# A graph network with attention on one core: the output's base traced behind the next softmax, and loads of bias rows tied to a step of the attention

## The chip, the cores and the metric

The kernel runs on one core of a Trainium2 chip. The metric is the device time of one execution in microseconds (us). A core has five engines that run their own instruction streams and wait for each other through semaphores: TensorE (PE, with its weight loads as PEld), VectorE (DVE), ScalarE (ACT), GpSimd (POOL) and SyncE (SP), which here issues nearly all DMAs and does nothing else. An engine takes its instructions in the order of the program, so one that waits holds up all that stand behind it on the same engine; on SP a DMA issue that waits holds up the issues behind it.

## The reference

What is computed is a graph network with pre-normalised attention over N = 1024 nodes of D = 512 features, in float32. Cut to what matters:

```
h = relu(layernorm(x))
x_in = h
h = batchnorm(h); h = gcn(h, gcn_in_w) + gcn_in_b
for i in range(4):
    a = attention(ln2(h), cond, Wq[i], Wk[i], Wv[i], Wo[i])   # 16 batches of 64 nodes, 256 keys each, 8 heads
    h = h + a
    val, gate = split(ln3(h) @ geglu_w[i] + geglu_b[i])
    h = h + (val * gelu(gate)) @ ffo_w[i] + ffo_b[i]
h = gcn(h, gcn_out_w) + gcn_out_b
return x + h + x_in
```

The change deals with two things of small arithmetic. One is the base of the output, `x + gcn_out_b + relu(layernorm(x))`, to which the last graph product is added at the very end. It doesn't depend on the layers, so it can be made at any time; two of its eight blocks of 128 nodes are made in each of the four layers. The other is the bias row `ffo_b[i]`, which is added to h once in each layer.

## The kernel before

The nodes are eight blocks of 128 (`h[0]` to `h[7]`). The attention of a layer runs over eight groups g of 128 nodes, two batches each. Products of large matrices are made from three products of twelve-bit parts: a left side x is split into a high part (`ah`, by ACT), a low part (`al`, by DVE) and a third (`as`, by POOL, in two halves); a bank of PSUM takes the first two products, ACT scales the bank, and then PE adds the third product. So the third product of each block k or v (L370) waits for ACT's scaling of its bank (L381).

In the loop over g, iteration g does, in the order of the source:

- `fetch_x`, in iterations 1 and 2 alone: loads a block of x again (`x_again`, L1550), and the first time in each layer also the row `bias_out` (by `load_row`, L136);
- the keys of group g + 1 and the mixing of group g, which turns its probabilities on PE (`tr_pr`), then the scores and the softmax of group g + 1 (`scores`): 32 small products into four banks, then for each bank the negative maximum `nmax` on DVE (L838), two exponentials on ACT (L843), a reciprocal and two scalings on DVE (L848). `scores.last` is the last of these scalings;
- the rest of mixing: `ol` and `os` on DVE (L892, L893), traced behind `scores.last` by `tc.issue_after`;
- `base_of`, in iterations 1 and 2 alone: `again` on ACT (L1556), two adds on DVE (L1558, L1559), and a store of the block to `base_dram` (L1560);
- the load of the condition of group g + 3 and its split for group g + 2 (`ah_c`, `al_c`, `as_c`), the values of group g + 1, and the output product of the attention of group g (`oy`, `ox`), which is added to `h[g]`. In layer 0 alone the condition is loaded raw in four pieces (`cond`, L270), turned on PE at the end of the iteration (`tr_cond`) and stored (`cond_dram`, L276) for the other layers, which load it turned (`ct`, L283).

Iteration 6 also loads the weights of the gated part (`wval`, `wgate`, L126), and `add_bias` loads the row `ffb` (L136) and adds it to h. POOL's sums of these weights (`ges`) wait for `scores.last`. The feed-forward part follows: gated products, whose results go to DRAM (`f_dram`), and the output product (`fy`, `fx`, L1252), which loads them back (`fr`) with the weights (`wff`).

The order in which the instructions stand on an engine is not that of the source. A scheduler makes it out of dependencies and of its own estimates, and may pull work ahead of where it was written. Three helpers bind it: `pin` keeps PE's products in program order; `tc.issue_after(i)` puts what is traced on the engine of i behind i, with no semaphore; `waiting_for(i, engine)` makes each instruction that is traced on that engine wait for i by a semaphore.

In the order that it makes, the first base block of a layer stands on DVE ahead of the softmax of group 1, in iteration 0, and the second inside or right behind that softmax, though both were written two iterations later. The loads of `bias_out` and `ffb` stand on SP much ahead too: those of layer 0 at the start of the program, those of layers 1 to 3 in the feed-forward part of the layer before.

Of the kernel before, what the change touches and what calls it, by code (L numbers as in the profile page):

```python
# [26 lines left out]
def gnn_kernel(  # L27
# [29 lines left out]
    N, D = x.shape  # L57
# [27 lines left out]
    @contextmanager  # L85
    def waiting_for(ins, engine):

        traced = nc.cur_bb.bb.instructions
        n = len(traced)
        yield  # L90
        for i in traced[n:]:
            if i.engine == engine:
                tc.add_manual_dep(i, ins.ins.name, mybir.DependencyInfo(
                    mybir.DependencyClass.Sync, mybir.DependencyReason.DATA))
# [36 lines left out]
    def three_halves(name):  # L131
        return rows.tile([P, 3 * D // 2], F32, tag="gs2", name=name, bufs=2)

    def load_row(vec, offset, name, t=None):
        t = three_halves(name)[:, :D] if t is None else t
        nc.sync.dma_start(  # L136
            t, bass.AP(tensor=vec.tensor, offset=vec.offset + offset, ap=[[0, P], [1, D]])
        )
        return t
# [665 lines left out]
    def acc_tile(name):  # L805
        return accs.tile([P, 512], F32, tag="acc", name=name)
# [13 lines left out]
    def scores(l, g, qT, kT):  # L820


        c0 = (g % 4) * P
        probs = {}
        banks = [bank(f"sc_{l}_{g}_{u}") for u in range(4)]
        for c2 in range(2):
            for a in range(2):
                for j in range(2):
                    pj = slice(j * DH, (j + 1) * DH)
                    for b in range(2):  # L830
                        pin(nc.tensor.matmul(
                            banks[2 * c2 + j][b * NPG:(b + 1) * NPG, a * M:(a + 1) * M],
                            qT[g // 4][c2][pj, a, c0 + b * NPG:c0 + (b + 1) * NPG],
                            kT[c2][pj, a, b * M:(b + 1) * M], start=True, stop=True))
        for u in range(4):
            ps3 = banks[u].rearrange("p (a m) -> p a m", a=2)
            nmax = small.tile([P, 2], F32, tag="nmax", name=f"nmax_{l}_{g}_{u}")
            nc.vector.tensor_reduce(nmax, ps3, AX.X, OP.max, negate=True)  # L838
            pr = t512(f"pr_{l}_{g}_{u}")
            pr3 = pr.rearrange("p (a m) -> p a m", a=2)  # L840
            tot = small.tile([P, 2], F32, tag="tot", name=f"tot_{l}_{g}_{u}")
            for a in range(2):
                nc.scalar.activation(pr3[:, a, :], ps3[:, a, :], AF.Exp,  # L843
                                     bias=nmax[:, a:a + 1], accum_out=tot[:, a:a + 1])
            inv = small.tile([P, 2], F32, tag="inv", name=f"inv_{l}_{g}_{u}")
            nc.vector.reciprocal(inv, tot)
            for a in range(2):
                scores.last = nc.vector.tensor_scalar(pr3[:, a, :], pr3[:, a, :], inv[:, a:a + 1],  # L848
                                                      None, OP.mult)
            probs[u] = pr  # L850
        return probs
# [85 lines left out]
    def load_geglu(l, r):  # L937
        return [load_w(geglu_w[l][:, r * D:(r + 1) * D], f"wval_{l}_{r}"),
                load_w(geglu_w[l][:, DFF + r * D:DFF + (r + 1) * D], f"wgate_{l}_{r}")]

    def geglu_weights(l, r, wval, wgate):
        s = slots_of(3, f"ges_{l}_{r}")
        sums_of_a(nc.gpsimd, *wval, *wgate, *s)
        return order7([*wval, *wgate], *s)
# [480 lines left out]
    for l in range(L):  # L1425
# [90 lines left out]
        def take_ln3():  # L1516
            ln3T.extend(slots_of(2, f"ln3T_{l}_{i}") for i in range(2))
            ln3S.extend(slots_of(3, f"ln3S_{l}"))
            right.extend([ln3T[0][0], ln3T[0][1], ln3T[1][1], ln3S[2], ln3S[0], ln3S[1],
                          ln3T[1][0]])  # L1520
# [22 lines left out]
        fetched = {}  # L1543

        def fetch_x(nb):
            if not fetched:
                fetched["bias"] = three_halves(f"bias_out_{l}")[:, :D]
                load_row(gcn_out_b, 0, "bias_out", fetched["bias"])
            fetched[nb] = acc_tile(f"x_again_{nb}")
            nc.sync.dma_start(fetched[nb], x[nb * P:(nb + 1) * P, :])  # L1550

        def base_of(nb):


            xt, bias_out, xn = fetched.pop(nb), fetched["bias"], acc_tile(f"again_{nb}")
            nc.scalar.activation(xn, xt, AF.Relu, bias=x_shift[:, nb:nb + 1],  # L1556
                                 scale=x_root[:, nb:nb + 1])
            nc.vector.tensor_tensor(xt, xt, bias_out, OP.add)  # L1558
            nc.vector.tensor_tensor(xt, xt, xn, OP.add)  # L1559
            nc.sync.dma_start(base_dram[nb], xt)  # L1560

        ffb = []

        def add_bias(t, *blocks):
            if not ffb:
                ffb.append(load_row(ffo_b, l * D, f"ffb_{l}"))
            for nb in blocks:
                t.tensor_tensor(h[nb], h[nb], ffb[0], OP.add)

# [11 lines left out]
        for g in range(NG - 1):  # L1581
            if g == NG - 2:
                take_ln3()
                raw = load_geglu(l, 0)
                add_bias(nc.vector)
            if not g:
                probs = scores(l, g, qT, kTs.pop(g))
            if g == NG - 2:
                with waiting_for(scores.last, mybir.EngineType.Pool):
                    left = geglu_weights(l, 0, *raw)  # L1590
            wo_flow = out_parts(l, wo) if not g else iter(())
            wo = next(wo_flow, wo)
            if g in (1, 2):
                fetch_x(2 * l + g - 1)
            k = keys(l, g + 1, wk, 1 if l == 0 and g == 0 else 0)
            for i, u in enumerate(k):
                u.begin()
                if not i:
                    for end in ends:
                        end()  # L1600
                if i > 1:
                    k[i - 2].end()
                next(wo_flow, None)
            k[-2].end()
            for _ in wo_flow:
                pass
            v = values(l, g + 1, wv)
            with in_order(mybir.EngineType.DVE) if g == NG - 2 else nullcontext():
                oT = mix(l, g, probs, vs.pop(g), (
                    k[-1].end, nothing, lambda: (v[0].begin(), g == NG - 2 and  # L1610
                                                 add_bias(nc.vector, *range(4)))))
            if g < NG - 2:
                probs = scores(l, g + 1, qT, kTs.pop(g + 1))
                with tc.issue_after(scores.last.ins):
                    oT = oT()
            if g == NG - 2:
                oT = oT()
                ln3_norm(g - 2, g - 1, behind=mix.last)
                add_bias(nc.gpsimd, g - 2, g - 1)
            if g in (1, 2):  # L1620
                base_of(2 * l + g - 1)
            if l == 0:
                fetch_cond(g + 3)
            split_cond(l, g + 2)
            if l:
                load_cond(l, g + 3)
            v[1].begin()
            v[0].end()
            v[2].begin()
            v[1].end()  # L1630
            pieces = attn_out(l, g, oT, wo, pin) if g < NG - 2 else iter(())
            next(pieces, None)
            if g in (3, 5):
                moments_into(mv_kept[:, 2 * (g - 3):2 * (g - 1)], [h[g - 3], h[g - 2]],
                             f"ln3_{l}_{g - 3}")
            if g == NG - 2:
                for nb in range(4):
                    ln3_turn(nb, each=pin)
            v[3].begin()
            next(pieces, None)  # L1640
            v[2].end()
            next(pieces, None)
            ends = [v[3].end]
            if g == NG - 3:
                scale_kept()
            if g == NG - 2:
                for nb in range(4, 6):
                    ln3_turn(nb, each=pin)
                for nb in (g - 2, g - 1):
                    ln3_sums(nc.gpsimd, nb)  # L1650
            if l == 0 and g + 3 < NG:
                turn_cond(g + 3, each=pin)
        g = NG - 1
        f, quads = quads_of(l, 0, left, right)
# [109 lines left out]
        for r in range(1, R):  # L1764
            f = Gated(l, r)
# [189 lines left out]
```

## Time and profile before

| | |
|---|---|
| median of 3 runs | 2304.32 us (2302.94 to 2304.63) |
| profiled execution, its own time | 2308.55 us |
| profiled execution, span of its instructions | 2306.8 us |
| mean granted clock of PE in it | 0.998 |
| DVE busy | 1738.5 us (75%) |
| ACT busy | 1169.6 us (51%) |
| POOL busy | 750.3 us (33%) |
| packets of SP's DMA queue | 25.8% of 16 engines' span |

The profile is of one execution on the chip, and its span starts at its first instruction. In a row of the order of time stand the start, the duration, the engine, the line of the kernel, the operation and the tiles that it writes and reads; xN counts merged instructions, and square brackets hold the idle time of the engine before it with what ended it. The ends of PE's products are modelled, so its busy time is not its peak. A row of a stretch has its length and each engine's busy time, with counts. A row of waits has the sum, the count and the longest.

### The profile page before, as it was taken

The numbers are of one execution on the slowest core, as the hardware profiler recorded it, in microseconds if no ns is written. First come the engines' busy times: TensorE is split into PE (matmuls) and PEld (weight loads), VectorE is DVE, ScalarE is ACT, GpSimd is POOL, SyncE is SP. The second block draws the span as 40 slices with busy tenths as digits, with TensorE's granted clock in tenths as the row PEclk, the third lists the DMA queues.
The fourth block names the chain that finished last, engine by engine and source line by source line (L and its number), as shares of the span: only waits on it lengthen the run. The fifth ranks groups of instructions, "written<-read, shape, count | busy, mean of one in ns | idle before, by whom it ended". The sixth has DMA issues, their size and how long they took to land. (4 is left out here: it accounts for less than half of the span.)

```text
span 2306.8 us, 34462 instructions
## 1 busy us (share of the span) xinstructions
PE 2271.7 (98%) x12496; PEld 1757.1 (76%) x12496; DVE 1738.5 (75%) x3172; ACT 1169.6 (51%) x2245; POOL 750.3 (33%) x647
## 2 busy tenths in 40 slices
PE   8999999999999999999999999999999999999999
PEld 5677887587887888488787888578788788668777
DVE  9886556999986556989987554989988554899965
ACT  7555445465355445465356444556437444556521
POOL 1121213486022224377022222368112113168301
PEclk9999999999999999999999999999999999999999
DMA  7042211234512101133522111133531111043551
GB/s 214 2 151 70 69 62 36 82 119 146 183 46 74 47 28 37 60 122 96 209 91 74 38 38 38 38 109 101 192 137 51 41 47 46 1 128 110 183 171 59
DMA packets 144114, 204.42 MB, mean 89 GB/s; under 512 B 11241, under 2 KB 68913, under 8 KB 143937
## 3 DMA queue, kind: packets, MB, share of 16 engines
q1 hardware_dynamic: 141840, 196.72, 25.8%
q0 software_dynamic: 1376, 4.30, 0.6%
q8 instruction: 103, 1.69, 0.3%
q10 hardware_dynamic: 720, 1.11, 0.1%
q14 instruction: 75, 0.61, 0.1%
HBM read 151.75 MB, written 50.34 MB: 88 GB/s over the span
## 5 line engine op out<-in xcount | busy, mean ns | idle before, releaser
L324 POOL TENSOR_TENSOR as_c<-ah_c,al_c 128x512 fp32r<-128x512 f32 x128 | 200.4, 1595 | 906.6 <-DVE al_c L319 711.3
L1123 ACT ACTIVATE g<-g 128x512 f32<-128x512 f32 x192 | 112.4, 585 | 152.3 <-PE g L1109 150.7
L381 ACT ACTIVATE k<-k 128x512 f32<-128x512 f32 x125 | 73.0, 586 | 197.9 <-PE k L370 197.9
L1252 PE MATMUL fy<-bl_wff,al_f 128*128 128x512 f32 x512 | 160.1, 392 | 1.3 <-DVE bl_wff L1229 0.8
L318 ACT ACTIVATE ah_f<-fr 128x1024 fp32r<-128x1024 f32 x64 | 67.9, 1061 | 183.7 <-PE fy L1252 90.7
L1252 PE MATMUL fx<-bs_wff,as_f 128*128 128x512 f32 x512 | 160.4, 393 | 0.6 <-DVE as_f L321 0.6
L1252 PE MATMUL fy<-bh_wff,ah_f 128*128 128x512 f32 x512 | 158.4, 391 | 0.2 <-ACT ah_f L318 0.2
L386 DVE COPY kT<-k 128x512 f32<-128x512 f32 x54 | 37.2, 689 | 156.6 <-PE k L370 156.6
L370 PE MATMUL v<-bs_wv,as_c 128*128 128x512 f32 x508 | 137.4, 393 | 7.2 <-ACT v L381 7.2
L370 PE MATMUL v<-bh_wv,ah_c 128*128 128x512 f32 x508 | 141.2, 400 | 0.0
L1050 POOL TENSOR_TENSOR gsa<-gha,gla 128x512 fp32r<-128x512 f32 x96 | 124.2, 1315 | 40.2 <-DVE gla L1045 40.2
L843 ACT ACTIVATE pr<-sc,nmax 128x256 f32<-128x256 f32 x256 | 118.2, 476 | 37.3 <-DVE nmax L838 36.7
L370 PE MATMUL v<-bl_wv,al_c 128*128 128x512 f32 x508 | 136.4, 390 | 0.0
L370 PE MATMUL k<-ah_c,bh_wk 128*128 128x512 f32 x500 | 135.0, 392 | 0.0
L381 ACT ACTIVATE v<-v 128x512 f32<-128x512 f32 x127 | 75.2, 592 | 116.9 <-PE v L370 116.9
L370 PE MATMUL k<-as_c,bs_wk 128*128 128x512 f32 x500 | 132.1, 395 | 1.7 <-ACT k L381 1.7
L370 PE MATMUL k<-al_c,bl_wk 128*128 128x512 f32 x500 | 133.7, 389 | 0.0
L1109 PE MATMUL g<-gr,gha 128*128 128x512 f32 x384 | 120.0, 394 | 0.0
L1109 PE MATMUL g<-gr,gsa 128*128 128x512 f32 x384 | 120.0, 394 | 0.0
L1109 PE MATMUL g<-gl,gla 128*128 128x512 f32 x384 | 118.3, 389 | 0.0
L370 PEld LDWEIGHTS v<-bs_wv,as_c 128*128 128x128 f32 x508 | 93.1, 188 | 32.4 <-ACT v L381 10.3
L1252 PEld LDWEIGHTS fy<-bl_wff,al_f 128*128 128x128 f32 x512 | 96.3, 188 | 24.5 <-DVE bl_wff L1229 3.7
(321 smaller groups left out, 5820.7 us busy)
## 6 DMA issues: line engine op xcount, KB each, us to landing
f_dram<-fT SPq DMA_DIRECT2D x128, 256.0 KB, 2.1
fr<-f_dram SPq DMA_DIRECT2D x64, 512.0 KB, 4.3
ct<-cond_dram SPq DMA_DIRECT2D x48, 512.0 KB, 4.9
wff<-in_L_gnn_ffo_w_dram SPq DMA_DIRECT2D x32, 512.0 KB, 6.9
gxb<-in_L_gnn_geglu_w_dram SPq DMA_DIRECT2D x96, 128.0 KB, 2.5
gxa<-in_L_gnn_geglu_w_dram SPq DMA_DIRECT2D x96, 128.0 KB, 2.5
cond<-in_L_gnn_cond_dram SPq DMA_DIRECT2D x32, 256.0 KB, 3.8
cond_dram<-ct SPq DMA_DIRECT2D x16, 512.0 KB, 3.3
```

The source lines that it names most:

```text
L318: nc.scalar.mul(twelve_bits(h), x, INWARD * TINY)
L324: nc.gpsimd.tensor_tensor(twelve_bits(s)[:, k, :], h[:, k, :], l[:, k, :], OP.subtract)
L370: pin(nc.tensor.matmul(self.bank, twelve_bits(left[k // 2])[:, k % 2, self.c * P:(self.c + 1) * P], twelve_bits(right[k // 2])[:, k % 2, : ...
L381: nc.scalar.mul(self.bank, self.bank, 1.0 + TINY)
L386: nc.vector.tensor_copy(self.to(), self.bank)
L843: nc.scalar.activation(pr3[:, a, :], ps3[:, a, :], AF.Exp, bias=nmax[:, a:a + 1], accum_out=tot[:, a:a + 1])
L1050: split_left.last = pin(t.tensor_tensor(s_at, h_at, l_at, OP.subtract))
L1109: pin(nc.tensor.matmul(to, self.part(i, which)[:, k, :], self.rights[i][which].bitcast(F32R)[:, k, :], start=start and k == 0, stop=stop a ...
L1123: pin(nc.scalar.mul(to, to, 1.0 + TINY))
L1252: pin(nc.tensor.matmul(to, twelve_bits(left[which][0])[:, k, b * P:(b + 1) * P], twelve_bits(right[which])[:, k, :], start=u == 0 and whic ...
```

## The change

Three places change, all in the attention. The issue of `bias_out` and that of `ffb` now wait, on SP, for the last instruction of the softmax traced last. And `base_of` is traced behind the last instruction of the softmax of the next group, on DVE; ACT's and SP's part of it isn't bound by that.

```diff
         def fetch_x(nb):
             if not fetched:
                 fetched["bias"] = three_halves(f"bias_out_{l}")[:, :D]
-                load_row(gcn_out_b, 0, "bias_out", fetched["bias"])
+                with waiting_for(scores.last, mybir.EngineType.SP):
+                    load_row(gcn_out_b, 0, "bias_out", fetched["bias"])
...
         def add_bias(t, *blocks):
             if not ffb:
-                ffb.append(load_row(ffo_b, l * D, f"ffb_{l}"))
+                with waiting_for(scores.last, mybir.EngineType.SP):
+                    ffb.append(load_row(ffo_b, l * D, f"ffb_{l}"))
...
             if g in (1, 2):
-                base_of(2 * l + g - 1)
+                with tc.issue_after(scores.last.ins):
+                    base_of(2 * l + g - 1)
```

No instruction is added or removed. On PE and POOL none stands elsewhere than before; on DVE, ACT and SP they move. DVE in layer 1, where `al_c` of group 2 leads to the softmax of group 1 (`nmax_1_0` is its first maximum), of the difference between the two orders:

```order
 L386 COPY kT_1_1_20973<-k_1_3_20978 128x512
 L319 SCALAR_TENSOR_TENSOR al_c_2_0_21145<-ah_c_2_0_21143,ct_2_0_20865 128x1024
-L1558 TENSOR_TENSOR x_again_21226<-x_again_21226,bias_out_21224 128x512
-L1559 TENSOR_TENSOR x_again_21226<-x_again_21226,again_21432 128x512
 L319 SCALAR_TENSOR_TENSOR al_c_2_1_21146<-ah_c_2_1_21144,ct_2_1_20866 128x1024
 L838 TENSOR_REDUCE nmax_1_0_21101<-sc_1_0_21081 128x2
```

The two adds of the first block left the place ahead of softmax 1. Those of the second block left the inside of softmax 1 (in layer 0 the place right behind it), and ACT's second `again` left it too, for a place in iteration 1; the first `again` stays ahead of softmax 1. The new place on DVE, behind softmax 2 (`pr_2_3` is its last scaling), again in layer 1:

```order
 L848 TENSOR_SCALAR pr_2_3_21422<-pr_2_3_21422,inv_2_3_21426 128x256 x2
 L892 SCALAR_TENSOR_TENSOR ol_1_21367<-oh_1_21366,po_1_21290 128x512
+L1559 TENSOR_TENSOR x_again_21226<-x_again_21226,bias_out_21224 128x512
 L893 TENSOR_TENSOR os_1_21368<-oh_1_21366,ol_1_21367 128x512
+L1560 TENSOR_TENSOR x_again_21226<-x_again_21226,again_21432 128x512
 L386 COPY v_2_0_21469<-v_2_1_21455 128x512
```

One add now stands between `ol` and `os`, one behind `os`; the second block's stand the same way behind softmax 3. On SP the rows of the changed kernel in layer 0, from the load of `bias_out` on, with the condition loads of groups 3 and 4:

```order
L136 DMA bias_out_16070<-in_L_gnn_gcn_out_b_dram 128x512
L270 DMA cond_0_15953<-in_L_gnn_cond_dram 128x512
L270 DMA cond_1_15954<-in_L_gnn_cond_dram 128x512
L270 DMA cond_2_15955<-in_L_gnn_cond_dram 128x512
L270 DMA cond_3_15956<-in_L_gnn_cond_dram 128x512
L276 DMA cond_dram<-ct_3_0_16040 128x1024
L276 DMA cond_dram<-ct_3_1_16041 128x1024
L270 DMA cond_0_16283<-in_L_gnn_cond_dram 128x512
L270 DMA cond_1_16284<-in_L_gnn_cond_dram 128x512
L1561 DMA base_dram<-x_again_16072 128x512
L270 DMA cond_2_16285<-in_L_gnn_cond_dram 128x512
L270 DMA cond_3_16286<-in_L_gnn_cond_dram 128x512
```

`bias_out` came here from the start of the program, ahead of four condition loads. The store of the first base block moved from ahead of `cond_0_15953` to between the loads of group 4; the load of the second x block stands right behind the last row, and its store between the condition loads of group 5 in the same way. In layers 1 to 3 `bias_out` stands ahead of the `ct` loads of group 4. In all layers `ffb` stands right ahead of the `wval` and `wgate` loads.

## Prediction

> **What bounds the kernel now.** I read the page first, then the waits of TensorE, then the stretches between score products, then the order of time inside one of them.
>
> ```profile
> span 2306.8 us, 34462 instructions
> PE 2271.7 (98%) x12496; PEld 1757.1 (76%) x12496; DVE 1738.5 (75%) x3172; ACT 1169.6 (51%) x2245; POOL 750.3 (33%) x647
> ```
>
> TensorE (PE) is busy for all but 35.1 us of the span, and the change leaves its order alone. So the change can only act through the moments in which PE waits, and can win at most a part of those 35.1 us, or add new ones.
>
> ```profile
> PE v L370 <- ACT v L381: 7.2, 5, 2.2
> ...
> PE fy L1252 <- DVE bl_wff L1229: 0.8, 2, 0.4
> ```
>
> The largest wait by far stands at one place: the third product of a v block waits until ACT has scaled that block's bank. Does it belong to the rows that the change moves? I cut each layer from the start of the scores of group 1 to those of group 2, and took the next group of layers 0 and 1 as the measure of an undisturbed stretch.
>
> ```profile
> 181.25:215.47 34.22, 32.53 (x241) 26.59 (x237) 21.32 (x39) 16.45 (x39) 7.01 (x6) 1.00 0.24 85
> 215.47:247.73 32.26, 32.26 (x239) 26.60 (x236) 16.13 (x34) 15.60 (x37) 5.62 (x4) 1.00 0.19 67
> 720.88:753.16 32.28, 30.76 (x225) 24.89 (x221) 19.50 (x34) 14.69 (x34) 6.76 (x5) 1.00 0.17 58
> 753.16:783.65 30.49, 30.49 (x224) 24.90 (x221) 15.67 (x30) 14.11 (x33) 5.99 (x5) 1.00 0.11 35
> 1251.55:1286.12 34.57, 32.35 (x225) 26.02 (x221) 19.51 (x34) 14.79 (x34) 6.76 (x5) 0.95 0.16 55
> 1784.08:1816.35 32.27, 30.75 (x225) 24.89 (x221) 19.47 (x34) 14.69 (x34) 6.75 (x5) 1.00 0.19 58
> ```
>
> The columns are the stretch, its length, then busy time of PE, weight load, DVE, ACT and POOL, the granted clock and the DMA. With the same work on PE, the stretch after softmax 1 is too long by 34.22 - 32.26 = 1.96 us in layer 0, and by 1.79, 4.08 and 1.78 us in layers 1 to 3 against 30.49: together 9.61 us, or 0.42% of the span. That is the purse. The 3.8 to 5.2 us more of busy DVE in the long rows hold the base adds and what they hinder. Layer 1 in order of time:
>
> ```profile
> 717.76 1.21 DVE L319 SCALAR_TENSOR_TENSOR al_c<-ah_c,ct 128x1024 fp32r<-128x1024 f32 x1
> ...
> 719.12 3.29 POOL L324 TENSOR_TENSOR as_c<-ah_c,al_c 128x512 fp32r<-128x512 f32 x2 [18.39 <-DVE al_c L319]
> 719.53 1.05 ACT L318 ACTIVATE ah_c<-ct 128x1024 fp32r<-128x1024 f32 x1
> 719.61 1.66 DVE L1559 TENSOR_TENSOR x_again<-x_again,again 128x512 f32<-128x512 f32 x1
> ...
> 720.88 1.96 PE L831 MATMUL sc<-kT,qT 64*64 64x256 f32 x32
> ...
> 721.19 2.29 DVE L319 SCALAR_TENSOR_TENSOR al_c<-ah_c,ct 128x1024 fp32r<-128x1024 f32 x1
> ...
> 723.41 1.27 DVE L838 TENSOR_REDUCE nmax<-sc 128x2 f32<-128x512 f32 x2
> ...
> 723.62 2.54 POOL L324 TENSOR_TENSOR as_c<-ah_c,al_c 128x512 fp32r<-128x512 f32 x2 [1.22 <-issue]
> ...
> 725.94 0.82 ACT L1556 ACTIVATE again<-x_again,x_shift,x_root 128x512 f32<-128x512 f32 x1
> ...
> 728.40 0.69 DVE L1559 TENSOR_TENSOR x_again<-x_again,again 128x512 f32<-128x512 f32 x1
> 728.44 0.63 ACT L381 ACTIVATE v<-v 128x512 f32<-128x512 f32 x1
> ...
> 729.12 1.20 PE L370 MATMUL v<-bs_wv,as_c 128*128 128x512 f32 x4 [1.52 <-ACT v L381]
> ```
>
> Two things delay softmax 1. Ahead of it the adds hold DVE until 721.27, so al_c ends at 723.48 and the first maximum starts at 723.41. Inside it ACT runs the second `again` for 0.82 us between the exponentials. The scaling of v stands behind the exponentials on ACT, so PE starts only at 729.12. The same work one group later, without the base:
>
> ```profile
> 753.16 1.96 PE L831 MATMUL sc<-kT,qT 64*64 64x256 f32 x32
> ...
> 754.29 1.29 DVE L838 TENSOR_REDUCE nmax<-sc 128x2 f32<-128x512 f32 x2 [1.45 <-PE sc L831]
> ...
> 758.95 0.59 ACT L381 ACTIVATE v<-v 128x512 f32<-128x512 f32 x1
> ...
> 759.36 0.62 DVE L848 TENSOR_SCALAR pr<-pr,inv 128x256 f32<-128x256 f32 x2
> ...
> 759.72 1.09 PE L370 MATMUL v<-bs_wv,as_c 128*128 128x512 f32 x4
> ```
>
> Here maximum to scaling takes 4.66 us, PE follows at scores + 6.56 and does not wait, though with only 759.72 - 759.54 = 0.18 us to spare. In softmax 1 the same distance was 5.03 us.
>
> **The change, layers 1 to 3.** The four adds leave this stretch, and the second `again` leaves ACT's softmax. The first `again` stays where it was on ACT, ahead of ah_c, so ah_c still ends at 720.58. Now al_c comes next on DVE. Does it run at once? Alone it took 1.21 us; beside POOL's as_c it took 2.29. POOL's pair alone takes 2.54, beside the adds 3.29. I read this as DVE and POOL taking turns, whole instructions at a time. Without the adds POOL's pair runs 719.12 to 721.66; al_c, ready at 720.6, waits for that, and ends at 721.66 + 1.21 = 722.87. The maximum starts 0.07 earlier, as in the trace, at 722.80 in place of 723.41. Then 4.66 to the scaling, 0.59 for it and 0.05 to PE: 728.10, against 729.12. **Gain 1.02 us** in layer 1; PE still comes later than 720.88 + 6.56 = 727.44, so some 0.77 of the 1.79 us stays. Layer 3 has the same rows: 1.02. If al_c need not wait for POOL, all 1.79 goes; if the order of turns is against it by one more half of as_c (1.27), nothing is won. I take the middle since 721.66 follows from the rows on both sides.
>
> Layer 2 lost more, for a second reason:
>
> ```profile
> 1257.76:1261.17 3.41, 1.19 (x6) 0.68 (x5) 3.33 (x12) 3.41 (x12) 0.00 (x0) 1.00 0.20 76
> 1261.17:1264.59 3.42, 3.42 (x10) 2.63 (x9) 1.79 (x3) 0.27 (x1) 0.00 (x0) 0.50 0.06 22
> ```
>
> Its wait left PE busy for 1.19 of 3.41 us, and in the next 3.42 us the granted clock was 0.50, which costs 1.71 us. With a stall like layer 1's rest this is gone: 4.08 - 0.77 = **3.31 us**. [...]
>
> **Layer 0.** Softmax 1 is relieved in the same way, but SP now stands still for it.
>
> ```profile
> 180.07 2.97 POOL L324 TENSOR_TENSOR as_c<-ah_c,al_c 128x512 fp32r<-128x512 f32 x2 [18.21 <-PE v L370]
> ...
> 189.65 1.20 PE L370 MATMUL v<-bs_wv,as_c 128*128 128x512 f32 x4 [1.69 <-ACT v L381]
> ...
> 196.21 1.91 PE L205 MATMUL tr_cond<-ident,cond 128*128 128x128 f32 x16
> ```
>
> POOL ends at 182.61, al_c at 183.82, the maximum starts at 183.75, and PE at 183.75 + 5.30 = 189.05: gain 0.60. But the load of bias_out waits on SP for the end of this softmax, 5.69 us after its maximum (759.98 - 754.29): 189.44. Four cond loads, which went out during this softmax, are behind it, and the transposes at 196.21 need them. The two kinds of row that size it are SP's pace (two loads in 0.92 us, so one in 0.46) and the landing of bias_out and of the load right behind it, in their earlier place:
>
> ```profile
> 752.86 0.92 SPq L283 DMA_DIRECT2D ct<-cond_dram  x2
> ...
> bias_out<-in_L_gnn_gcn_out_b_dram SPq DMA_DIRECT2D x1, 256.0 KB, 4.9
> ...
> fr<-f_dram SPq DMA_DIRECT2D x1, 512.0 KB, 5.9
> ```
>
> bias_out took 4.9 us, and the 512 KB of fr landed 5.9 + 0.46 - 4.9 = 1.46 us after it: 0.7 per 256 KB. So the conds land at 195.1, 195.8, 196.5 and 197.2, and the four blocks of transposes, now due at 195.6 with 0.44 between, wait 0.3 in the end. **Net gain 0.3**; bounds 0.6 (loads in time) and -1 (each 0.3 later).
>
> In groups 1 and 2 of layer 0 the store of the base now stands between the second and the third cond load. Softmax 2 ends 6.82 after 215.47, at 222.3; ol, add, os, add at about 0.65 each end at 224.9; the store goes then, the third load at 225.3.
>
> ```profile
> 228.47 1.91 PE L205 MATMUL tr_cond<-ident,cond 128*128 128x128 f32 x16
> ...
> cond<-in_L_gnn_cond_dram SPq DMA_DIRECT2D x4, 256.0 KB, 3.6
> ...
> DMA to landing us min/median/max: 2.0/3.3/7.0
> ```
>
> It is needed at 228.47 + 0.88 = 229.35, so 4.0 us are there for 3.6 (the last row is x_again's, with its stores): cost 0 by the median, some 3 us by the slowest.
>
> **What costs nothing.** Behind softmax 2 and 3 os comes one add (0.69) later and the copy of v two; in PE's order four groups of four products, each about as long as the 1.09 us of the last row of softmax 2, stand between the time at which os was made and the product that reads it, and that is the cover; without it each group would lose the 0.7 of one add. The waits for bias in layers 1 to 3 hold the ct loads of group 4, but these go at 752.86 anyway, long after softmax 1. The ffb load waits for softmax 6, and the four geglu loads stand behind it. POOL needs them:
>
> ```profile
> 884.34 2.40 POOL L243 TENSOR_TENSOR ges<-wgate,wgate 128x1024 f32<-128x1024 f32 x1 [5.86 <-DMA wgate<-in_L_gnn_geglu_w_dram]
> ...
> 911.99 2.77 POOL L1568 TENSOR_TENSOR hall<-hall,ffb 128x512 f32<-128x512 f32 x2 [17.96 <-DVE xn_ln L193]
> ```
>
> POOL's first sum waits for that softmax as well, so it had ended by 884.34. At the latest ffb lands 4.9 later and the loads 4 x 1.4 after that, at 894.9 (an estimate from the rows of bias_out and fr), and POOL is through 9.7 later, at 904.6, with its next work at 911.99: 0. Without that cover a later POOL would hold up the gated products.
>
> The two row loads also leave the queue of the feed-forward part, where PE lost 0.8 us in two waits on ffo weights. I count 0.7 for that; its bounds are 0 and 0.8.
>
> **Sum.** 0.3 + 1.02 + 3.31 + 1.02 + 0.7 = 6.35 us, so the profiled span would fall from 2306.8 to 2300.4. That execution took 2308.55 us by its own time, 4.2 above the median 2304.32, so its half-clock stretch of layer 2 and the late load before it (3.31 - 1.02 = 2.29) may not be in every run. I take off half of that: 5.2, and forecast 2304.32 - 5.2 = **2299.1**.
>
> **The rivals.** (1) The stalls vanish altogether, because al_c gets in ahead of POOL's second half: 9.6 + 0.7 - 1.15 = 9.15, 2295.2. For it: the undisturbed softmax has no wait. Against it: the first `again` still delays ah_c past POOL's start. (2) The gain is mostly handed back in layer 0 (-1 there, 0.3 in each later group), with no half-clock in layer 2 to win and no gain in the feed-forward part: 3.06 - 1.6 = 1.5, 2302.8. (3) The change doesn't do what it says: al_c waits one more half of as_c, and softmax 1 is as late as before: 2304. (4) Slower: in layer 0 the loads behind SP's new waits land later than PE bears. From 2.2 us of waiting (a landing over 6.2 us in groups 1 and 2, where 7.0 occurs) the clock halves too: 2.2 + 1.7 = 3.9 at each of three places, 11.7, less the 4.9 that stay from the other terms: 2311.1. Against it: the median of 3.6.
>
> **Chances.** Forecast 0.58, (1) 0.12, (2) 0.15, (3) 0.07, (4) 0.08. The forecast's own range is 2297.5 to 2300.7; 0.2% (4.6 us) is about what a measurement of this kernel can tell from no change, and two thirds of the forecast lie beyond it. Faster by over 0.2%: 0.38 + 0.12 = 0.50; within: 0.20 + 0.15 + 0.07 = 0.42; slower: 0.08. The range of 8 in 10 reaches from near (1) past (2): 2295.5 to 2303.5.
>
> **What would show it.** Right: the stretches after softmax 1 at 31.2 us in layers 1 to 3 with a rest of 0.6 or so of waiting for ACT's v and a clock of 1.00, al_c ending 1.2 after POOL's pair, the first maximum 1.9 after the scores' start; in layer 0 some 33.9, with transposes that wait for a cond load by less than 1 us. Wrong: full waits for v in spite of the moved adds, waits of tr_cond over 1 us or a half clock in layer 0, PE waiting in groups 2 and 3 for os or for a bank, or gated products that wait for POOL's sums.

## The result, and the profile after

The changed kernel took 2297.64 us (median of 10 runs, 2295.83 to 2298.53) against 2304.31 us before (10 runs, 2302.33 to 2305.24): a ratio of 0.9972, with a 95% interval from 0.9964 to 0.998. That is 6.7 us faster; 5.2 were forecast. The profiled execution took 2296.64 us by its own time. Its page begins:

```profile
span 2294.9 us, 34482 instructions
PE 2265.4 (99%) x12496; PEld 1754.5 (76%) x12496; DVE 1734.6 (76%) x3172; ACT 1168.7 (51%) x2245; POOL 747.1 (33%) x647
```

Between the two profiled executions the span fell by 11.9 us, nearly twice what the medians say. The lines below show which part is the change. Among the waits of TensorE (total, times, longest) the place that the forecast named is down from 7.2 to 2.6 us, and a wait for `bl_wff` is no longer among them:

```profile
PE v L370 <- ACT v L381: 2.6, 5, 1.0
```

The stretches from the scores of group 1 to those of group 2, layers 0, 1, 2 and 3, with the undisturbed stretch of layer 1 in the middle (columns as in the prediction):

```profile
179.14:212.67 33.53, 32.55 (x240) 26.59 (x236) 18.86 (x35) 15.88 (x38) 6.56 (x6) 1.00 0.22 72
717.31:748.57 31.26, 30.80 (x224) 24.89 (x220) 17.56 (x31) 14.10 (x33) 5.99 (x5) 1.00 0.14 43
748.57:779.06 30.49, 30.49 (x224) 24.91 (x220) 16.79 (x32) 14.80 (x34) 5.96 (x5) 1.00 0.17 52
1246.12:1277.38 31.26, 30.80 (x225) 24.89 (x221) 17.56 (x31) 14.10 (x33) 5.99 (x5) 1.00 0.13 44
1774.84:1806.08 31.24, 30.78 (x225) 24.89 (x221) 17.56 (x31) 14.10 (x33) 5.98 (x5) 1.00 0.13 43
```

They lost 0.69, 1.01, 3.31 and 1.03 us. The output products of the feed-forward part lost time too. Their windows before, layers 0 to 3, and then after:

```profile
566.17:654.85 88.68, 88.33 (x386) 71.92 (x385) 82.64 (x108) 29.44 (x30) 8.91 (x4) 1.00 0.53 189
1096.76:1185.52 88.76, 88.36 (x386) 71.92 (x385) 82.64 (x108) 29.45 (x30) 8.91 (x4) 1.00 0.53 189
1629.66:1718.05 88.39, 88.36 (x386) 71.92 (x385) 82.64 (x108) 29.46 (x30) 8.91 (x4) 1.00 0.53 190
2160.05:2251.63 91.58, 90.20 (x386) 73.01 (x385) 67.48 (x79) 29.96 (x33) 4.29 (x8) 0.98 0.58 194
```

```profile
563.50:651.25 87.75, 87.75 (x386) 72.10 (x385) 82.64 (x108) 29.43 (x30) 8.91 (x4) 1.00 0.51 181
1092.25:1180.04 87.79, 87.78 (x386) 72.08 (x385) 82.64 (x108) 29.34 (x30) 8.91 (x4) 1.00 0.51 181
1620.99:1708.81 87.82, 87.82 (x386) 72.10 (x385) 82.65 (x108) 29.33 (x30) 8.91 (x4) 1.00 0.51 181
2149.68:2239.73 90.05, 88.68 (x386) 71.86 (x385) 67.47 (x79) 29.95 (x33) 4.29 (x8) 1.00 0.57 199
```

That is 0.93, 0.97, 0.57 and 1.53 us. The program's start, up to the first scores, fell from 165.37 to 163.22 us. These three groups make 6.04 + 4.00 + 2.15 = 12.2 us; the other stretches changed by at most 0.11 us each and gave back 0.3 together.

Inside layer 1 the rows stand as follows, in order of time:

```profile
713.29 0.84 ACT L1557 ACTIVATE again<-x_again,x_shift,x_root 128x512 f32<-128x512 f32 x1
715.46 0.58 ACT L381 ACTIVATE v<-v 128x512 f32<-128x512 f32 x1 [1.34 <-PE v L370]
715.55 2.52 POOL L324 TENSOR_TENSOR as_c<-ah_c,al_c 128x512 fp32r<-128x512 f32 x2 [18.42 <-DVE al_c L319]
715.96 1.05 ACT L318 ACTIVATE ah_c<-ct 128x1024 fp32r<-128x1024 f32 x1
717.04 2.11 DVE L319 SCALAR_TENSOR_TENSOR al_c<-ah_c,ct 128x1024 fp32r<-128x1024 f32 x1 [1.64 <-ACT ah_c L318]
717.31 1.96 PE L831 MATMUL sc<-kT,qT 64*64 64x256 f32 x32
719.07 1.28 DVE L838 TENSOR_REDUCE nmax<-sc 128x2 f32<-128x512 f32 x2
723.85 0.59 ACT L381 ACTIVATE v<-v 128x512 f32<-128x512 f32 x1
724.50 1.21 PE L370 MATMUL v<-bs_wv,as_c 128*128 128x512 f32 x4 [0.47 <-ACT v L381]
```

The first maximum starts at scores + 1.76 (2.53 before), maximum to scaling takes 4.78 us, and PE waits 0.47 us in place of 1.52. Two things are left to explain: `al_c` still takes 2.11 us, ending 1.08 us after POOL's pair (715.55 + 2.52 = 718.07), and in front of it ACT makes `ah_c` only after a `v` scaling for which it sat idle for 1.34 us.

### The profile page after: what moved, and what is told of

It reads as the page before. It is cut to its first block, busy times and chain, and to the rows that moved or that the text cites. A ratio compares the mean times of both kernels' runs of the same rounds, so it can differ in the third digit from the quotient of the medians.

```text
span 2294.9 us, 34482 instructions
## 1 busy us (share of the span) xinstructions
PE 2265.4 (99%) x12496; PEld 1754.5 (76%) x12496; DVE 1734.6 (76%) x3172; ACT 1168.7 (51%) x2245; POOL 747.1 (33%) x647
## 5 line engine op out<-in xcount | busy, mean ns | idle before, releaser
L370 PEld LDWEIGHTS v<-bh_wv,ah_c 128*128 128x128 f32 x508 | 92.6, 188 | 27.9 <-issue 9.2
```

The lines of the kernel that those rows point to most:

```text
L370: pin(nc.tensor.matmul(self.bank, twelve_bits(left[k // 2])[:, k % 2, self.c * P:(self.c + 1) * P], twelve_bits(right[k // 2])[:, k % 2, : ...
```

## The experiments

The theory at this point: the adds of the base delayed softmax 1 from two sides, and the binding moved them; the row loads cost time by themselves in the feed-forward part. Rivals: one edit is worth all, or the extra 5 us between the traces are chance.

Each ratio is against runs of the kernel before in the same round. Their medians were 2304.31 us for the change, 2303.7 for the loads, the base, the second block and the change with the split, 2304.4 for the two single rows, and 2305.42 for the last row, so rows of different rounds are compared by their ratios.

| kernel | median us (runs) | ratio to before, 95% interval | stretch after softmax 1, layer 1 | output products, layer 0 |
|---|---|---|---|---|
| before (first trace) | 2304.31 (10) | 1 | 32.27 | 88.68 |
| the change | 2297.64 (10) | 0.9972 [0.9964, 0.998] | 31.26 | 87.75 |
| loads alone | 2296.57 (6) | 0.9966 [0.9954, 0.9979] | 31.22 | 87.76 |
| base alone | 2298.76 (9) | 0.9977 [0.9967, 0.9987] | 31.26 | 88.41 |
| the change, base bound for the second block only | 2297.83 (10) | 0.9972 [0.9963, 0.9982] | 31.26 | 87.78 |
| output bias row alone | 2297.26 (8) | 0.9973 [0.9962, 0.9983] | 31.25 | 87.80 |
| feed-forward bias row alone | 2302.23 (10) | 0.9989 [0.9979, 0.9998] | 32.29 | 87.77 |
| change, split earlier | 2293.05 (5) | 0.9953 [0.9939, 0.9966] | 30.52 | 87.81 |
| output bias row, split earlier | 2293.21 (5) | 0.9949 [0.9935, 0.9962] | 30.49 | 87.78 |

**The loads alone.** The change without the binding of the base:

```diff
             if g in (1, 2):
-                with tc.issue_after(scores.last.ins):
-                    base_of(2 * l + g - 1)
+                base_of(2 * l + g - 1)
```

> The two bias rows are loaded at their own step, as in the change; the output's base stays where it was before. Theory (the row loads in the queue cost time by themselves, at the program's start and in the feed-forward part): the stretches from the scores of group 1 to those of group 2 stay at 34.2, 32.3, 34.6 and 32.3 us (layer 2 at 32.3 to 32.6 if its half-clock stretch does not come again); the output products of the feed-forward part get shorter by 0.9, 1.0 and 0.6 us in layers 0 to 2; the stretch from the start to the first scores falls from 165.4 to about 163.2. Time: 2304.3 - 2.5 - 2.1 = 2299.7. Rival (the start and the feed-forward part differed by chance, the loads are worth the 0.7 us of the forecast): both stay within 0.3 of before, 2303.6.

Measured: 2296.57 us, and the stretches after softmax 1 fell as with the whole change, to 33.53, 31.22, 31.25 and 31.25 us. Both sides of the expectation had them unchanged, and both were wrong there. The order of DVE in this kernel against the one before shows why, in layer 1 behind softmax 1:

```
 TENSOR_TENSOR os_0<-oh_0,ol_0 128x512
 COPY v_1_0<-v_1_1 128x512
+TENSOR_TENSOR x_again<-x_again,bias_out 128x512
+TENSOR_TENSOR x_again<-x_again,again 128x512
```

The first add reads `bias_out`. With its load waiting for the end of softmax 1, the order that the scheduler makes has the adds behind softmax 1, with no binding. The trace has them there too, and the first waits for the load:

```profile
721.00 1.28 DVE L838 TENSOR_REDUCE nmax<-sc 128x2 f32<-128x512 f32 x2
726.42 1.20 PE L370 MATMUL v<-bs_wv,as_c 128*128 128x512 f32 x4 [0.47 <-ACT v L381]
729.84 0.69 DVE L1559 TENSOR_TENSOR x_again<-x_again,bias_out 128x512 f32<-128x512 f32 x1 [1.12 <-DMA bias_out<-in_L_gnn_gcn_out_b_dram]
```

In the feed-forward part the output products took 87.76, 87.78 and 87.79 us in layers 0 to 2, as the theory had it. The start stayed at 165.52 us, against the theory, so its 2.1 us are not a gain of the loads.

**The base alone.** The change with both loads early, as before:

```diff
-                with waiting_for(scores.last, mybir.EngineType.SP):
-                    load_row(gcn_out_b, 0, "bias_out", fetched["bias"])
+                load_row(gcn_out_b, 0, "bias_out", fetched["bias"])
...
-                with waiting_for(scores.last, mybir.EngineType.SP):
-                    ffb.append(load_row(ffo_b, l * D, f"ffb_{l}"))
+                ffb.append(load_row(ffo_b, l * D, f"ffb_{l}"))
```

> The output's base is traced behind the next softmax, as in the change; the bias rows are loaded early, as before. Theory: the stretches after softmax 1 fall by 0.7, 1.0, 3.3 and 1.0 us to 33.5, 31.3, 31.3 and 31.3 with a rest of 0.5 us of waiting for v in layers 1 to 3; the start (165.4) and the output products of the feed-forward part stay as before. Time: 2304.3 - 3.7 = 2300.6, and 2298.3 if layer 2's half clock was in the runs of before. Rival (the start and the feed-forward part gained through the base, or by chance of the clock): they are shorter here too, and the time is that of the whole change, 2297.6.

Measured: 2298.76 us; stretches of 33.51, 31.26, 31.25 and 31.26 us, output products of 88.41, 88.35, 88.51 and 91.59 us. The theory holds: the binding gains the stretches and not the feed-forward part. Either edit alone moves the adds; only the loads free the output products.

**Only the second block bound.** The binding for `g == 2` alone, with both loads moved.

> As the change, but only the second of the two base blocks of a layer is traced behind its softmax; the first keeps its old place, with its two adds ahead of the first maximum. Theory (two delays that add: 0.61 ahead of the softmax by the adds, 0.4 inside it by the second activation): the first maximum starts 2.5 us after the scores as before, the distance from maximum to scaling falls from 5.03 to 4.7, and the stretches of layers 1 and 3 are 31.9 us. In layer 0, where the second block lay behind the softmax before, 34.2. Time: the change's 2297.6 + 3 x 0.6 + 0.7 = 2300.1. Rival A (all of the gain comes from the adds ahead): stretches of 32.3, 2301.4. Rival B (all of it from the activation inside): stretches of 31.3, 2297.6.

Measured: 2297.83 us, 31.26 us in layer 1. The number fits rival B, but the run does not test it: with the load of `bias_out` waiting, the adds of the first block leave softmax 1 too. The two delays had to be separated with the loads left early.

**One delay at a time.** The kernel before, with only the second block of the base moved, that is its activation and, behind it, its two adds:

```diff
-                nc.scalar.activation(pr3[:, a, :], ps3[:, a, :], AF.Exp,
+                scores.exp = nc.scalar.activation(pr3[:, a, :], ps3[:, a, :], AF.Exp,
...
-                base_of(2 * l + g - 1)
+                with tc.issue_after(scores.exp.ins) if g == 2 else nullcontext():
+                    base_of(2 * l + g - 1)
```

> The kernel before with one thing changed: the activation of a layer's second base block is bound behind the exponentials of softmax 3, and its two adds follow. Nothing else leaves its place. Theory (two delays that add up in softmax 1): the adds ahead still hold the first maximum at scores + 2.5, the activation inside is gone and maximum to scaling is 4.66 in place of 5.03, so the stretches after softmax 1 are 31.9 us in layers 1 and 3. In softmax 3 the activation now stands right ahead of the scaling of v, which had 0.18 us to spare: PE waits 0.82 - 0.18 = 0.64 us there. Rival (softmax 1 is paced by DVE, so the activation inside costs nothing): 32.3 us after softmax 1. Rival in softmax 3 (other slack covers it): no wait for v.

Measured: 31.99 us in layers 1 to 3, so the activation inside softmax 1 cost 0.28 us, and the adds ahead the other 31.99 - 31.25 = 0.74. The second block's own adds left with the activation, but in the kernel before they stand behind the last maximum on DVE (from 727.69 us on; it ends at 727.25), so they held up no exponential. In softmax 3 the reverse was to be seen:

```profile
720.64:752.63 31.99, 30.77 (x224) 24.89 (x221) 18.32 (x32) 14.12 (x33) 6.75 (x5) 1.00 0.16 50
783.12:814.32 31.20, 30.78 (x224) 24.89 (x220) 16.82 (x32) 14.81 (x34) 5.96 (x5) 1.00 0.22 75
```

```profile
788.92 0.81 ACT L1556 ACTIVATE again<-x_again,x_shift,x_root 128x512 f32<-128x512 f32 x1
789.62 0.59 ACT L381 ACTIVATE v<-v 128x512 f32<-128x512 f32 x1
790.27 1.20 PE L370 MATMUL v<-bs_wv,as_c 128*128 128x512 f32 x4 [0.42 <-ACT v L381]
```

The activation right ahead of the scaling lengthened that stretch from 30.49 to 31.20 us: 0.71 for an expected 0.64. The recorded wait of PE is only 0.42 of it. A stretch between two markers sees the whole loss, a wait line a part.

**One row load at a time.** First only the wait of `bias_out`, then only that of `ffb`.

> Only the load of the output's bias row waits for its step; the feed-forward bias row goes early and the base stays where it was in the text. The run with both loads moved and the base left had the whole gain, so theory: the adds of the base cannot start before their bias row has landed, and the waiting load alone moves them out of softmax 1: stretches of 31.2 to 31.3 us in layers 1 to 3. The output products of the feed-forward part stay near 88.5 us in layers 0 to 2, since the row that stands among their weight loads is the other one. Rival (any one row less in the queue is enough): 87.8 us there too.

> Only the load of the feed-forward bias row waits for its step; the output's bias row goes early and the base stays. Theory: the output products of the feed-forward part take 87.8 us in layers 0 to 2 as with the whole change, and the stretches after softmax 1 stay at 34.2, 32.3, 32.9 and 32.3 us (layer 2: 34.6 if a half-clock stretch follows its wait again). Time: 2304 - 2.5 = 2301.5. Rival (both rows together made the weights late, or the bias row did): 88.3 us or more there.

With `bias_out` alone: 2297.26 us, stretches of 31.25 to 31.26 us in layers 1 to 3, output products of 87.80, 87.83 and 87.80 us. That is the whole gain of the change, from one line. The rival's number came out, but not for its reason: SP takes its issues in order (in the kernel before `fr` goes out at 566.82, behind an `ffb` that had waited for 2.9 us, as the rows below show), and in this kernel `ffb` stands behind the waiting load, in the attention, so it left the feed-forward part too. With `ffb` alone: 2302.23 us, output products of 87.76, 87.78 and 87.79 us and stretches of 34.20, 32.29, 32.95 and 32.27 us, as the theory had it. There `bias_out` still goes out at 557.11 and costs nothing that shows. That `ffb` in its old place with `bias_out` gone would cost the same was not tried.

The chain in the feed-forward part of layer 0, in the kernel before:

```profile
566.43 0.34 SPq L136 DMA_DIRECT2D ffb<-in_L_gnn_ffo_b_dram  x1
573.17 1.06 ACT L318 ACTIVATE ah_f<-fr 128x1024 fp32r<-128x1024 f32 x1 [3.95 <-DMA fr<-f_dram]
574.26 1.23 DVE L319 SCALAR_TENSOR_TENSOR al_f<-ah_f,fr 128x1024 fp32r<-128x1024 f32 x1 [1.14 <-ACT ah_f L318]
578.06 0.69 DVE L1229 SCALAR_TENSOR_TENSOR bl_wff<-wff,bh_wff 128x512 fp32r<-128x512 f32 x1
578.80 0.50 PE L1252 MATMUL fy<-bl_wff,al_f 128*128 128x512 f32 x1 [0.35 <-DVE bl_wff L1229]
```

and with `ffb` gone:

```profile
568.83 1.06 ACT L318 ACTIVATE ah_f<-fr 128x1024 fp32r<-128x1024 f32 x1 [1.72 <-DMA fr<-f_dram]
570.93 1.22 DVE L319 SCALAR_TENSOR_TENSOR al_f<-ah_f,fr 128x1024 fp32r<-128x1024 f32 x1
574.72 0.69 DVE L1229 SCALAR_TENSOR_TENSOR bl_wff<-wff,bh_wff 128x512 fp32r<-128x512 f32 x1
```

Read from the top: `ffb` goes out at 566.43 and the load of `fr` only behind it, 0.65 us after the first output product (566.17). Without `ffb` that load goes out 2.57 us before it (561.48 against 564.05). SP had stood still in front of `ffb`. The first row is that wait (total, times, longest), the two others are the load of `fr` in the kernel before and with `ffb` gone:

```profile
SPq L136 <- PE g L1109: 2.9, 1, 2.9
566.82 0.42 SPq L1211 DMA_DIRECT2D fr<-f_dram  x1
561.48 0.52 SPq L1211 DMA_DIRECT2D fr<-f_dram  x1
```

The row is loaded into one of a pair of buffers that parts of the gated weights use too (`three_halves` in the kernel), so its issue waits until PE is through with the last gated products, and the issues behind it on SP wait with it. The transfer of `fr` itself took no longer beside the row: 6.3 us from issue to landing, against 7.3 without it. ACT waits 3.95 us for this `fr` where it waited 1.72 without the row; DVE takes its work in order: it idles for 1.14 us ahead of `al_f`, until 574.26, and `bl_wff`, which stands behind it and had its data (`bh_wff` ends at 575.17), starts only at 578.06 and comes late for PE, which waits 0.35 us for it. The wait line names `bl_wff`; what was late is `fr`, and what made it late is a row load that waited for a buffer.

**The rest of the stall.** The changed kernel, with the split of the condition's group 2 traced earlier:

```diff
+            if not g:
+                split_cond(l, 2)
             v = values(l, g + 1, wv)
...
-            split_cond(l, g + 2)
+            if g:
+                split_cond(l, g + 2)
```

> As the change, but the split of the condition's group 2 is traced ahead of the first v block, so that ACT makes the second ah_c before it scales that v block, and al_c comes on DVE before POOL's pair. Theory (what is left of the stall is al_c waiting for POOL's pair): al_c runs at once, the first maximum starts 1.1 us after the scores as in the undisturbed softmax, the stretches after softmax 1 are 30.5 us in layers 1 to 3 and 32.3 in layer 0, and the time is 2297.6 - 3 x 0.77 - 1.26 = 2294.0. Rival (al_c waits its turn beside POOL in any order, or the earlier ah_c delays the copies of the probabilities): the stretches stay at 31.3 or grow, and the time is 2297.6 or more.

Measured: 2293.05 us, and the stretches are free of waits, 32.25, 30.52, 30.50 and 30.52 us:

```profile
181.52:213.77 32.25, 32.25 (x240) 26.62 (x237) 17.60 (x35) 15.59 (x37) 5.20 (x4) 1.00 0.21 74
718.37:748.89 30.52, 30.52 (x224) 24.93 (x221) 15.84 (x31) 14.10 (x33) 5.20 (x4) 1.00 0.13 44
```

```profile
714.35 1.08 ACT L318 ACTIVATE ah_c<-ct 128x1024 fp32r<-128x1024 f32 x1
714.91 2.53 POOL L324 TENSOR_TENSOR as_c<-ah_c,al_c 128x512 fp32r<-128x512 f32 x2 [16.73 <-DVE al_c L319]
716.48 2.04 DVE L319 SCALAR_TENSOR_TENSOR al_c<-ah_c,ct 128x1024 fp32r<-128x1024 f32 x1
717.01 0.81 ACT L1557 ACTIVATE again<-x_again,x_shift,x_root 128x512 f32<-128x512 f32 x1
719.50 1.29 DVE L838 TENSOR_REDUCE nmax<-sc 128x2 f32<-128x512 f32 x2 [0.97 <-PE sc L831]
```

`ah_c` now ends at scores - 2.94 in place of scores - 0.30, and the maximum waits for the scores alone. `al_c` is no faster: 2.04 us, ending 1.08 us after POOL's pair once more. It only starts early enough. The theory was right in time and stretches and wrong on the way: `al_c` did not run at once and did not come ahead of POOL's pair.

**The smallest edit.** The kernel before with the wait of `bias_out` and this split, and nothing else; and beside it the changed kernel on the same chip:

> The smallest edit that the runs so far point to: the kernel before, with the load of the output's bias row waiting for its step, and the split of the condition's group 2 traced ahead of the first v block. The wait for the feed-forward bias row and the binding of the base are left out. Theory (those two add nothing once the bias row waits): stretches of 30.5 us after softmax 1 in layers 1 to 3 and 32.3 in layer 0, output products of the feed-forward part at 87.8 us, and 2293 us, the time of the whole change with the split moved. Rival (the binding keeps the adds out of the way of something that the earlier split needs): stretches above 31 us or longer groups behind them, 2296 or more.

> The changed kernel unchanged, so that the next one can be held against it on the same chip. Both theories: 2297.6, with stretches of 33.5, 31.3, 31.3 and 31.3 us after softmax 1; the trace may hold half-clock stretches of 1.7 us at the start, near 2215 us, or none.

Measured: 2293.21 us against 2296.91 us of the changed kernel, 5 runs each, and 2305.42 us before. Its stretches are 32.25, 30.49, 30.51 and 30.51 us. Against their own kernel before, it is as fast as the whole change with the split moved (0.9949 and 0.9953), so the wait of `ffb` and the binding add nothing to it that shows.

**The kernel before, once more,** for a second trace of it.

> The kernel before, unchanged, for another execution's trace. Theory (half-clock stretches come from the place at which a fixed grid of 3.41 us falls over the same waits, and that place differs by execution): the undisturbed parts of the stretches repeat within 0.1 us (32.3 us in layers 1 and 3, 32.9 or 34.6 in layer 2, 88.7, 88.8 and 88.4 us in the feed-forward parts of layers 0 to 2), while at least one of the three half-clock stretches of the first trace (at 87.0, 1261.2 and 2223.7 us) is missing or stands elsewhere, each with 1.7 us. Rival (they belong to the program): the same three at the same places.

Measured: one execution of 2302.05 us with a span of 2300.3, 6.5 below the first trace of the same kernel. None of the three half-clock stretches came again: the stretch of layer 2 took 32.32 us in place of 34.57, the output products of layer 3 took 90.03 in place of 91.58, and the start 163.21 in place of 165.37. In the second trace of the changed kernel, the other way round, a half-clock stretch stood in layer 3's output products, which took 91.58 us. So these 1.7 us pieces belong to the execution. Two sizes were missed here. The stretch of layer 2 was expected at 32.9 or 34.6 us; in the first trace the second `again` had waited 0.6 us for its block `x_again`, and here it didn't. The output products of layers 0 and 1 took 88.18 and 88.44 us where 88.7 and 88.8 were expected: in layer 0 the late `fr` took 5.8 us from issue to landing and not 6.3.

## Why the prediction was right, point by point

**What bounds the kernel** was read rightly at its main place: the two views that decided it (PE's wait for `v`, and stretches against an undisturbed one) showed the gain where it came. One step was wrong: that the change could win only idle time of PE. Of the 11.9 us between the first traces 5.6 came out of idle time (35.1 to 29.5 us), and 6.3 out of busy time (2271.7 to 2265.4 us), since products at half clock (3.42 of 3.42 us busy at 0.50 in layer 2), and products behind late weight loads (one recorded at 0.50 us in place of 0.39 in layer 0), count as busy.

**Layers 1 and 3: 1.02 each forecast, 1.01 and 1.03 measured.** The two parts came out as 0.74 by the adds ahead (forecast 1.02 - 0.37 = 0.65) and 0.28 by the activation inside (0.37). Both are off by 0.09 us, in opposite directions, so that the sum fits to 0.01 is luck. The turns with POOL were read rightly: `al_c` ended 1.08 us after POOL's pair in the changed kernel, 1.08 after it with the split moved, and 1.07 before (723.48 against 722.41). What it waits for is not the pair, but the one sum that is running when it comes. In the changed kernel these are POOL's second sum ahead of softmax 1, and then the next group in order of time:

```profile
716.80 1.27 POOL L324 TENSOR_TENSOR as_c<-ah_c,al_c 128x512 fp32r<-128x512 f32 x1
745.88 1.28 POOL L324 TENSOR_TENSOR as_c<-ah_c,al_c 128x512 fp32r<-128x512 f32 x1 [24.05 <-DVE al_c L319]
746.26 1.98 DVE L319 SCALAR_TENSOR_TENSOR al_c<-ah_c,ct 128x1024 fp32r<-128x1024 f32 x1
747.12 2.25 POOL L324 TENSOR_TENSOR as_c<-ah_c,al_c 128x512 fp32r<-128x512 f32 x1
```

In the next group `al_c` came during the first sum, ended 1.08 us after it (748.24 against 747.16), and the second sum took 2.25 us in place of 1.27. So they take turns, as the prediction read it. Ahead of softmax 1 `al_c` came at 717.04, 0.24 us after the second sum had started; by that much it missed the turn that the first rival gave it.

**Layer 2: 3.31 forecast and 3.31 measured between the two first traces.** Against the second trace of the kernel before it is 32.32 - 31.26 = 1.06 us, the same as in the layers beside it; the rest is the half clock (1.71) and a later load of `x_again` (0.5). That 3.31 was met is the luck of which executions were traced; taking off half of 2.29 us against the median was the right kind of step.

**Layer 0: 0.3 net forecast, 0.69 measured.** The relief of 0.60 was there. The 0.3 to be handed back was not: PE has no wait for the transposes of the condition in the changed kernel, so the loads behind SP's new wait landed in time. That was the upper bound of 0.6, and it fell short by 0.1.

**The feed-forward part: 0.7 forecast with bounds of 0 and 0.8; measured 2.47 in layers 0 to 2 between the first traces, and 0.43 + 0.65 + 0.58 = 1.66 against the second trace of before.** This is the term that was mis-sized, and its upper bound was wrong. It took PE's two recorded waits as all the loss. In layer 0 PE's row shows 0.35 us of waiting, the window 0.93: the loss also stands in late weight loads (0.77 and 0.43 us of waiting on PEld at that place), behind which PE counts as busy, with a product recorded at 0.50 us in place of 0.39. The windows of layers 0 to 2 against each other could not show it, since all three were late.

**What stays of the stall, 0.77 per layer,** was forecast rightly in size (31.26 against 30.49) and wrongly in cause. The step said that the first `again` delays `ah_c`. In the rows of the changed kernel `again` is through at 714.13, and then ACT idles until 715.46 for the `v` scaling that stands ahead of `ah_c`. With `ah_c` ahead of that scaling, and `again` moved with it, the stall was gone.

**A step that was not asked.** The prediction took the binding as what moves the adds, and the loads as a risk. The waiting load alone moves them, since the add reads what it brings. The sum was not touched by that, because both edits were in the change.

**The start** (2.1 us between the traces) was not forecast and is not the change: it is 163.21 in the second trace of before and 165.52 us with the loads alone. The first trace of before holds a half-clock stretch of 3.41 us at 87.0 us (granted clock 0.50), which is 1.7 of the 2.1.

**The sum.** Between the two traces without half-clock stretches (spans 2300.3 and 2294.9) the change is worth 5.4 us: 3.8 in softmax 1 (0.66 + 1.01 + 1.06 + 1.03) and 1.7 in the output products. The forecast of 5.2 is near this partly by luck: it had 0.96 too little in the feed-forward part and 0.36 in layer 0, and 1.1 more in layer 2 than the 1.06 that repeat.

The medians differ by 6.7. Part of the other 1.3 us is the half clock. By an estimate from 3.41 us at 0.50 in some 2300 us, one such stretch takes 0.0007 off a run's mean granted clock, which is on record for each run of the experiments: in the round that ran both side by side, 4 of 5 runs of the changed kernel stand at 1.000, and none of 9 before; in all rounds with this record 8 of 15 against 11 of 45. So these stretches do fall less often with the change. But the runs at 1.000 took 2302.67 us before and 2296.42 after, by their means over different chips, which is still 6.25 apart. What the rest is isn't shown; the lateness of `fr`, which made 0.8 us between the two traces of before, is a candidate.

**The rivals.** Stalls that vanish altogether did not come with this change; they came with the split, through an earlier `ah_c`, and even there `al_c` did not get ahead of POOL's second sum. The gain handed back in layer 0, the change without effect, and late loads behind SP's waits were not seen: from the scores of group 2 to those of group 7 no layer changed by more than 0.11 us.

## What to carry to other kernels

A wait on a load also moves whatever reads its data: look at the whole order of an engine, and take the edits of a change apart before crediting one. A load whose issue waits, for a buffer or for a step, also holds up the loads behind it (2.9 us here): look for the wait in front of an issue before blaming its bytes. Measure a stall as the length of a stretch against an undisturbed one, since a wait line shows only part of it (0.42 of 0.71 us, 0.35 of 0.93) and names the last link and not the late one. When a stall shrinks but stays, find what stands ahead of its first link on that engine: here one split traced a few lines earlier was worth 3.7 us, and one waiting load was as good as the whole change.

## What the hardware showed that was not expected

In the first trace of the kernel before the half-clock stretches stand whole steps of 3.41 us apart. Each takes 3.41 us at a granted clock of 0.50, and they start at 86.99, 1261.18 and 2223.73 us: the gaps of 1174.19 and 962.55 us are 344 and 282 steps of 3.4133 us. In the second trace of the same kernel none of the three came again. Two traces with the same waits in the output products of layer 3, one with and one without a half clock; first the second trace of the changed kernel:

```profile
2209.18:2212.59 3.41, 2.04 (x7) 1.07 (x7) 2.45 (x2) 0.25 (x1) 0.00 (x0) 1.00 1.09 373
2212.59:2216.00 3.41, 3.41 (x9) 2.65 (x9) 1.61 (x2) 1.06 (x1) 0.00 (x0) 0.50 0.99 358
```

and then the second trace of the kernel before:

```profile
2215.89:2219.30 3.41, 2.25 (x7) 1.27 (x8) 2.45 (x2) 0.16 (x1) 0.00 (x0) 1.00 1.11 405
2219.30:2222.71 3.41, 3.41 (x17) 2.82 (x15) 2.44 (x2) 0.90 (x1) 0.00 (x0) 1.00 1.03 371
```

The three waits there are short: in the first trace of the kernel before they took 0.24, 0.53 and 0.60 us, 1.37 together. Where all three fell into the 3.41 us right ahead of a half-clock stretch, PE was busy for 2.04 us of them and the next 3.41 us ran at 0.50; in the 3.41 us of the other trace PE was busy for 2.25, so a little of the waits fell outside, and the clock stayed at 1.00. So no single long gap is needed. Nor does PE's busy time alone decide it: in the first trace of the kernel before two stretches of 3.41 us in softmax 1, whole steps away from the half-clock ones, had PE busy for only 1.99 and 1.89 us (185.98 to 189.39 and 1790.24 to 1793.65 us), and the clock stayed at 1.00 behind both. What does decide stays open. The prediction's fourth rival had the clock halve from 2.2 us of waiting; here 1.37 us in three waits came ahead of a half clock.
